# Graph network edge loops: streamed loads and stores for two chunks of edges at a time

## The chip, the cores and the metric

The kernel runs on one core of one Trainium2 chip. The metric is the device time of one execution in microseconds (us). Several executions are timed and the median is given. One further execution is recorded by the hardware profiler; its page and its trace are what is read here. A difference of about 0.2% (21 us) is what a measurement of this kernel can tell from no change.

## The reference

The reference computes two graph layers after one another on 10000 nodes with 64 features and 160000 edges that are sorted by their target node `dst`. The first is a GENConv stack of four layers with a softmax per target node and feature, the second is one attention layer. Cut to what matters:

```
h  = relu(layernorm(x));  x0 = h @ encW + encb;  ea = edge_attr @ eencW + eencb
genconv(x):                                   # four times, with layernorm and relu between
    m      = relu(x[src] + ea) + 1e-7
    logits = m * t
    e      = exp(logits - segment_max(logits, dst)[dst])
    agg    = segment_sum(m * e / segment_sum(e, dst)[dst], dst)
    return mlp(agg + x)
x = x + genconv stack(h)
attention:                                    # once
    score  = exp(clip(sum_per_head(K[src] * Q[dst] / sqrt(8) * E), -5, 5))
    x      = x + segment_sum(V[src] * score, dst)
```

The inputs are float32.

## The kernel before

**Tiling.** The sorted edge list is cut in the middle. The first half runs forwards on partitions 0 to 63 and the second half runs backwards on partitions 64 to 127, so one column of a tile holds one edge of each half, with 64 features each. A group is 128 columns and a chunk is four groups, 512 columns; 80000 columns make 158 chunks, of which the last three are shorter (`chunks`, `NC`). Sums and maxima per target node are scans along the columns; a row of marks in bfloat16 tells where a node's edges end or go on.

**Stages.** After a setup (encoder, marks, indices) come four softmax layers (`softmax_layer`, numbered 0 to 3), each followed by a node layer, then the attention layer and a last pass of gathers. Each softmax layer and the attention layer is one loop over the 158 chunks, in which most of the time lies. Between them the node layer gathers one row per node from the states (`n_g`) and builds the next table.

**One chunk of a softmax layer.** `front(k)` issues eight gathers on POOL (L650, 128 rows each, tile `xg` with seven buffers); multiplies the edge features on PE into the PSUM tile `z` (L734, three buffers) and adds the gathered rows in four further matmuls (L736); ACT turns `z` into logits (L739, L740); DVE scans them with the marks (L746) and subtracts (L748); ACT makes exponentials (L751 to L754, L761). `back(k)`, which is called one chunk later, makes two more scans on DVE (L774, L776, L779), transposes the results into the tile `so` (L805) and stores it in four transfers on SP's queue (L809).

**What is streamed on SP's queue.** `fetch(k + 2)` is called at the start of round `k`: the marks in two transfers (L709, five buffers) and the edge features `ea` in one (L660, three buffers). So one chunk of layers 1 to 3 issues seven transfers in this order: marks, marks, `ea` of chunk k+2, then four stores of chunk k-1. In layer 0 the edge features come as rows in two transfers (`er`, L667 and L669), are turned on PE (`turn_rows`, L678, L679), copied by ACT (L682) and written out as `eaT` (L683), which makes nine transfers.

**The attention layer** has the same form: `fetch_kv` issues eight gathers on POOL (`kv`, L650, in the same seven buffers as `xg`), `fetch(k + 2)` loads queries `q` (L1035), marks and `ea`; `ahead`, `scores`, `weights` and `back` compute, and `back` stores four transfers (L1110): eight transfers a chunk.

**What sets the order.** `InOrder` makes every engine run its instructions in the order in which the program issues them. Waits between engines are semaphores that the framework places. A transfer's completion counts on one of eight semaphores of its queue in turn, and each transfer waits until the transfer eight before it has landed.

Of the kernel before, what the change touches and what calls it, by code (L numbers as in the profile page):

```python
# [16 lines left out]
P = 128  # L17
# [4 lines left out]
CG = 4  # L22
# [4 lines left out]
def kernel(ctx: ExitStack, tc: tile.TileContext, a, out):  # L27
# [22 lines left out]

    chunks = [(g, CG) for g in range(0, NG - 5, CG)] + [(NG - 5, 2), (NG - 3, 2), (NG - 1, 1)]
    NC = len(chunks)
    W = 1280
    R = NE // W
    KT = W // P
# [617 lines left out]
    def turn_rows(k, er):  # L673

        g0, n, cols = span(k)
        pt = ps("ept", [P, CE])
        for g in range(n):
            nc.tensor.matmul(pt[:D, g * G:(g + 1) * G], er[:, 0, g, :], ident, start=True, stop=True)  # L678
            nc.tensor.matmul(pt[D:, g * G:(g + 1) * G], er[:, 1, n - 1 - g, :], anti,  # L679
                             start=True, stop=True)  # L680
        ea = edge.tile([P, CE], F32, name="ea", bufs=3)
        nc.scalar.activation(ea[:, :n * G], pt[:, :n * G], AF.Copy)  # L682
        nc.sync.dma_start(eaT[:, cols], ea[:, :n * G])  # L683
        return ea

    class InOrder:
# [14 lines left out]
                self.last[ins.engine] = ins  # L701
            self.seen = len(self.block.instructions)

    def load_marks(k, rows):

        g0, n, cols = span(k)
        t = edge.tile([P, CE], BF, name="marks", bufs=5)
        for s in range(2):
            nc.sync.dma_start(t[s * D:(s + 1) * D, :n * G], rows[s:s + 1, cols].to_broadcast([D, n * G]))  # L709
        return t  # L710
# [3 lines left out]
    def softmax_layer(l, ea_rows=None):  # L714
# [5 lines left out]
            numbers = ps("oe", [P, P])  # L720
            V.tensor_copy(numbers, iota_row)

        def fetch(k):
            return load_marks(k, ends_d), load_ea(k) if ea_rows is None else load_rows(k, ea_rows)

        def front(k, marks, ea):
            g0, n, cols = span(k)
            m = n * G
            xg = edge.tile([P, CG, 2, D], F32, name="xg", bufs=7)
            for g in range(n):  # L730
                for s in range(2):
                    gather(xg[:, g, s, :], tables[l], index(g0 + g, s))
            z = ps_a([P, CE])
            nc.tensor.matmul(z[:, :m], eencW, ea[:, :m], start=True, stop=False)  # L734
            for g in range(n):
                nc.tensor.matmul(z[:, g * G:(g + 1) * G], xg[:, g, :, :].rearrange("p s d -> p (s d)"),  # L736
                                 ident, start=False, stop=(g == n - 1))
            lg = ps("lg", [P, CE])
            S.activation(lg[:, :m], z[:, :m], AF.Relu)  # L739
# [30 lines left out]
        def back(k, z, u, dec, e):  # L770
# [35 lines left out]
            rows_out = st0[2 * g0 * G:2 * (g0 + n) * G, :].rearrange(  # L806
                "(b e s) (h x) -> s h e b x", e=32, s=2, h=2)
            for q in range(4):
                nc.sync.dma_start(rows_out[q // 2, q % 2],  # L809
                                  so[q * 32:(q + 1) * 32, :m // 32].rearrange("p b i c -> p b (i c)"))  # L810

        order = InOrder()
        got = [fetch(k) for k in range(2)]
        ea = got[0][1] if ea_rows is None else turn_rows(0, got[0][1])
        held, counts = None, []
        for k in range(NC):
            if k + 2 < NC:
                got.append(fetch(k + 2))
            z, u, up, e = front(k, got[k][0], ea)
            if k + 1 < NC:  # L820
                ea = got[k + 1][1] if ea_rows is None else turn_rows(k + 1, got[k + 1][1])
# [12 lines left out]
    def node_layer(l):  # L834
# [193 lines left out]
    def attention_layer():  # L1028

        prev = {}  # L1030

        def fetch(k):
            g0, n, cols = span(k)
# [3 lines left out]
            return load_marks(k, keeps_d), q, load_ea(k)  # L1037

        def ahead(k, keep, q, ea):

            g0, n, cols = span(k)
            m = n * G
            pq = ps("oe", [P, CE])
            for g in range(n):
                nc.tensor.matmul(pq[:, g * G:(g + 1) * G], q[:, g, :, :].rearrange("p s d -> p (s d)"),  # L1045
# [43 lines left out]
        def back(k, keep, pv, sc):  # L1089
            g0, n, cols = span(k)  # L1090
            m = n * G
            wv = ps("lg", [P, CE])
# [12 lines left out]
            so = edge.tile([P, CE // 32, 32], F32, name="so1", tag="so", bufs=3)  # L1105
            V.transpose(so[:, :m // 32, :], s[:, :m].rearrange("p (b e) -> p b e", e=32))
            rows_out = st1[2 * g0 * G:2 * (g0 + n) * G, :].rearrange(
                "(b e s) (h c) -> s h e b c", e=32, s=2, h=2)
            for q in range(4):
                nc.sync.dma_start(rows_out[q // 2, q % 2], so[q * 32:(q + 1) * 32, :m // 32])  # L1110

        order = InOrder()
        got = [fetch(k) for k in range(2)]
        made = ahead(0, *got[0])
        held = None
        for k in range(NC):
            kvs = fetch_kv(k)
            if k + 2 < NC:
                got.append(fetch(k + 2))
# [3 lines left out]
            held = got[k][0], pv, weights(k, psc)  # L1123
            if k + 1 < NC:
                made = ahead(k + 1, *got[k + 1])
            order()
        back(NC - 1, *held)
        order()
# [72 lines left out]
```

## Time and profile before

| | us |
|---|---|
| median of 3 runs | 10540.5 (10537.92 to 10543.13) |
| profiled execution, its own time | 10552.99 |
| its span on the core | 10551.1 |

The span by stage, from the first gather of each loop to its last, in windows of the trace (us):

| stage | window | length | POOL busy | DVE busy | PE busy | ACT busy |
|---|---|---|---|---|---|---|
| layer 0 | 160.6 to 2263.0 | 2102.4 | 1182.5 | 1241.8 | 832.2 | 622.4 |
| layer 1 | 2501.5 to 4270.7 | 1769.2 | 1182.2 | 921.4 | 565.3 | 540.6 |
| layer 2 | 4492.8 to 6262.7 | 1769.9 | 1182.2 | 922.1 | 565.5 | 540.9 |
| layer 3 | 6485.7 to 8258.9 | 1773.2 | 1182.3 | 921.1 | 563.6 | 540.1 |
| attention | 8616.6 to 10406.5 | 1789.9 | 1183.4 | 901.6 | 871.2 | 96.3 |

How to read it: the profiled execution took 12.5 us more than the median, so a sum that is made in the trace is taken to the median by leaving out 12.5 us. PE is TensorE, PEld its weight loads, DVE VectorE, ACT ScalarE, POOL GpSimd, SP SyncE; "SPq" marks a transfer that SP issues. An engine that is busy for half of a stage can still be the one that sets its length, when it also needs time between its instructions. "Remote" as the releaser of a wait means that the profile found no instruction or transfer that ended just then.

### The profile page before, as it was taken

How to read it: one execution, taken by the hardware profiler on the slowest of the kernel's cores; microseconds unless marked ns; L12 is line 12 of the kernel's file. 1: busy time of each engine (PE TensorE's matmuls, PEld its weight loads, DVE VectorE, ACT ScalarE, POOL GpSimd, SP SyncE). 2: the span in 40 equal slices, each digit the busy share in tenths (PEclk: the TensorE clock that was granted, in tenths of full speed). 3: DMA queues.
4: the chain of work that ended last, by engine and by line, in shares of the span. 5: the costliest groups of instructions: out<-in, count | busy, mean ns of one | idle time of the engine just before them, and what ended most of it. 6: DMA issues, size and time to landing. Idle time of an engine off the chain costs nothing. (4 is left out here: it accounts for less than half of the span.)

```text
span 10551.1 us, 67713 instructions
## 1 busy us (share of the span) xinstructions
PE 3999.8 (38%) x15722; PEld 2664.3 (25%) x15722; DVE 5487.0 (52%) x7537; ACT 2806.8 (27%) x4787; POOL 6367.8 (60%) x6736
## 2 busy tenths in 40 slices
PE   2433444344333333423333334233333355454452
PEld 1322322222222222212222222122222233333332
DVE  3666666642555555435555552555555445555553
ACT  1323333333333333423333333233333320000000
POOL 2555555545666666466666655666666456666665
PEclk8666666666555555655655556555555667777776
DMA  3545555454444444334444442444444325555553
GB/s 104 109 105 109 109 108 107 107 145 119 99 104 106 104 103 105 78 76 104 104 104 103 107 108 53 94 106 104 102 104 106 78 69 130 123 130 126 123 127 83
DMA packets 2467719, 1103.64 MB, mean 105 GB/s; under 512 B 2047265, under 2 KB 2239911, under 8 KB 2467088
## 3 DMA queue, kind: packets, MB, share of 16 engines
q1 hardware_dynamic: 2252120, 827.12, 33.5%
q0 software_dynamic: 215200, 272.11, 12.0%
q8 instruction: 140, 2.29, 0.1%
q14 instruction: 259, 2.12, 0.1%
HBM read 626.48 MB, written 471.91 MB: 104 GB/s over the span
## 5 line engine op out<-in xcount | busy, mean ns | idle before, releaser
L650 POOL DMA_INDIRECT xg<-table,idxA x2500 | 2364.8, 946 | 2198.2 <-issue 706.1
L734 PE MATMUL z<-ea,eencW 128*128 128x512 f32 (+1 forms) x1264 | 1271.0, 1108 | 4869.2 <-ACT ea L682 988.9
L650 POOL DMA_INDIRECT xg<-table,idxB x2500 | 2364.5, 946 | 763.6 <-issue 760.2
L746 DVE TENSOR_TENSOR_SCAN u<-lg,u,marks 128x512 f32<-128x512 f32 (+1 forms) x628 | 798.8, 1272 | 2962.3 <-ACT lg L740 2185.9
L734 PEld LDWEIGHTS z<-ea,eencW 128*128 128x128 f32 x1264 | 311.9, 306 | 5012.4 <-issue 2087.2
L736 PEld LDWEIGHTS z<-ident,xg 128*128 128x128 f32 x5000 | 1204.3, 329 | 747.6 <-issue 725.1
L736 PE MATMUL z<-ident,xg 128*128 128x128 f32 x5000 | 1186.1, 415 | 94.3 <-DMA xg<-table,idxB 77.5
L739 ACT ACTIVATE lg<-z 128x512 f32<-128x512 f32 (+1 forms) x632 | 356.8, 565 | 2689.1 <-remote 2112.7
L650 POOL DMA_INDIRECT kv<-kv_table,idxA x625 | 591.2, 946 | 414.9 <-remote 212.6
L776 DVE TENSOR_TENSOR_SCAN se<-dec,se,e 128x512 f32<-128x512 f32 (+1 forms) x628 | 791.9, 1261 | 0.0
L779 DVE TENSOR_TENSOR_SCAN sm<-dec,sm,me 128x512 f32<-128x512 f32 (+1 forms) x628 | 781.9, 1245 | 0.0
L751 ACT ACTIVATE up<-lg 128x512 f32<-128x512 f32 (+1 forms) x632 | 374.4, 592 | 1306.3 <-DVE lg L748 701.7
L650 POOL DMA_INDIRECT kv<-kv_table,idxB x625 | 591.2, 946 | 191.1 <-issue 189.3
L1079 PE MATMUL dec<-eq,head_sum 128*128 128x512 f32 (+2 forms) x316 | 238.0, 844 | 919.2 <-DVE eq L1077 879.9
L650 POOL DMA_INDIRECT n_g<-st,ends x316 | 301.9, 955 | 430.2 <-DMA marks<-ends_d 107.8
L1086 ACT ACTIVATE sc<-sc 128x512 f32<-128x512 f32 (+1 forms) x158 | 98.7, 625 | 1724.9 <-DVE sc L1085 660.4
L761 ACT ACTIVATE dec<-up 128x512 f32<-128x512 f32 (+1 forms) x632 | 376.8, 596 | 644.3 <-issue 540.0
L740 ACT ACTIVATE lg<-lg,teps,tcol 128x512 f32<-128x512 f32 (+1 forms) x632 | 471.8, 747 | 21.0
L1050 DVE TENSOR_TENSOR_SCAN qh<-marks,qh,oe 128x512 f32<-128x512 bf16 (+1 forms) x157 | 198.4, 1264 | 519.9 <-remote 429.2
L748 DVE TENSOR_TENSOR lg<-lg,u 128x512 f32<-128x512 f32 (+1 forms) x632 | 438.1, 693 | 22.0
L805 DVE STREAM_TRANSPOSE so<-se 128x512 f32<-128x512 f32 (+1 forms) x632 | 429.3, 679 | 0.0
L774 DVE SCALAR_TENSOR_TENSOR me<-z,e 128x512 f32<-128x512 f32 (+1 forms) x632 | 426.0, 674 | 0.0
(270 smaller groups left out, 6592.0 us busy)
## 6 DMA issues: line engine op xcount, KB each, us to landing
st<-so SPq DMA_DIRECT2D x2480, 128.0 KB
ea<-eaT SPq DMA_DIRECT2D x620, 256.0 KB
marks<-ends_d SPq DMA_DIRECT2D x1240, 64.0 KB
st<-so SPq DMA_DIRECT2D x652, 64.0 KB
xg<-table,idxA POOLq DMA_INDIRECT x2500
xg<-table,idxB POOLq DMA_INDIRECT x2500
qs<-zeros SPq DMA_DIRECT2D x156, 256.0 KB
er<-in_edge_attr_dram SPq DMA_DIRECT2D x310, 128.0 KB
```

The lines of the kernel that those rows point to most:

```text
L650: nc.gpsimd.indirect_dma_start(out=t, out_offset=None, in_=table, in_offset=bass.IndirectOffsetOnAxis(ap=idx, axis=0))
L734: nc.tensor.matmul(z[:, :m], eencW, ea[:, :m], start=True, stop=False)
L736: nc.tensor.matmul(z[:, g * G:(g + 1) * G], xg[:, g, :, :].rearrange("p s d -> p (s d)"), ident, start=False, stop=(g == n - 1))
L740: S.activation(lg[:, :m], lg[:, :m], AF.Identity, bias=teps[:, l:l + 1], scale=tcol[:, l:l + 1])
L746: V.tensor_tensor_scan(u[:, 1:m + 1], lg[:, :m], marks[:, :m], last, op0=OP.max, op1=OP.add)
L748: V.tensor_sub(lg[:, :m], lg[:, :m], u[:, 0:m])
L751: S.activation(up[:, :m], lg[:, :m], AF.Relu)
L761: S.activation(dec[:, :m], up[:, :m], AF.Exp, scale=-1.0)
L774: V.scalar_tensor_tensor(me[:, :m], z[:, :m], 0.0, e[:, :m], op0=OP.max, op1=OP.mult)
L776: V.tensor_tensor_scan(se[:, :m], dec[:, :m], e[:, :m], prev.get("e", zero1), op0=OP.mult, op1=OP.add)
L779: V.tensor_tensor_scan(sm[:, :m], dec[:, :m], me[:, :m], prev.get("m", zero1), op0=OP.mult, op1=OP.add)
L805: V.transpose(so[:, :m // 32, i, :], t[:, :m].rearrange("p (b e) -> p b e", e=32))
```

## The change

Chunks are joined to units of two (`units`, `unit_of`); the last two chunks are units of their own, so there are 80 units. The tiles of marks, edge features, rows, queries and stored states become twice as wide. `fetch` is called once for a unit, at the first chunk of the unit before it. `back` transposes each chunk into its half of `so` and issues the four stores at the last chunk of a unit; `turn_rows` does the same with the `eaT` store. Buffers, in units: marks three (from five chunks), `ea` three (from three chunks), `er` and `q` two (from three chunks), `so` two (from three chunks). The node layer's tile `n_g` takes the place of `ea` instead of that of `so`. The arithmetic and the gathers are as before, and the bytes of the transfers too.

For two chunks the transfers are: softmax layers 1 to 3 seven instead of fourteen, layer 0 nine instead of eighteen, attention eight instead of sixteen, each of twice the size.

```diff
+    units = [[k, k + 1] for k in range(0, NC - 2, 2)] + [[NC - 2], [NC - 1]]
+    unit_of = {k: u for u, ks in enumerate(units) for k in ks}
...
+    def reach(u):
+        g0 = chunks[units[u][0]][0]
+        n = sum(chunks[k][1] for k in units[u])
+        return g0, n, slice(g0 * G, (g0 + n) * G)
+    def within(k):
+        c = (chunks[k][0] - chunks[units[unit_of[k]][0]][0]) * G
+        return slice(c, c + chunks[k][1] * G)
...
-    def load_ea(k):
-        g0, n, cols = span(k)
-        ea = edge.tile([P, CE], F32, name="ea", bufs=3)
+    def load_ea(u):
+        g0, n, cols = reach(u)
+        ea = edge.tile([P, 2 * CE], F32, name="ea", bufs=3)
         nc.sync.dma_start(ea[:, :n * G], eaT[:, cols])
         return ea
-    def load_rows(k, ea_rows):
-        g0, n, cols = span(k)
-        er = edge.tile([P, 2, CG, D], F32, name="er", bufs=3)
+    def load_rows(u, ea_rows):
+        g0, n, cols = reach(u)
+        er = edge.tile([P, 2, 2 * CG, D], F32, name="er", bufs=2)
...
-        nc.scalar.activation(ea[:, :n * G], pt[:, :n * G], AF.Copy)
-        nc.sync.dma_start(eaT[:, cols], ea[:, :n * G])
+        nc.scalar.activation(ea[:, in_unit], pt[:, :n * G], AF.Copy)
+        if is_last(k):
+            nc.sync.dma_start(eaT[:, unit_cols], ea[:, :total * G])
...
-        t = edge.tile([P, CE], BF, name="marks", bufs=5)
+        t = edge.tile([P, 2 * CE], BF, name="marks", bufs=3)
...
-            so = edge.tile([P, CE // 32, 2, 32], F32, name="so", bufs=3)
+            if is_first(k):
+                prev["so"] = edge.tile([P, 2 * CE // 32, 2, 32], F32, name="so", bufs=2)
+            so, to = prev["so"], within(k)
             for i, t in ((0, se), (1, sm)):
-                V.transpose(so[:, :m // 32, i, :], t[:, :m].rearrange("p (b e) -> p b e", e=32))
+                V.transpose(so[:, to.start // 32:to.stop // 32, i, :],
+                            t[:, :m].rearrange("p (b e) -> p b e", e=32))
+            if not is_last(k):
+                return
...
-        got = [fetch(k) for k in range(2)]
+        got = [fetch(0)]
         for k in range(NC):
-            if k + 2 < NC:
-                got.append(fetch(k + 2))
-            z, u, up, e = front(k, got[k][0], ea)
+            if is_first(k) and unit_of[k] + 1 < len(units):
+                got.append(fetch(unit_of[k] + 1))
+            z, u, up, e = front(k, got[unit_of[k]][0], ea)
...
-            my["g"] = t = edge.tile([P, GRP, D2], F32, name="n_g", tag="so", bufs=3)
+            my["g"] = t = edge.tile([P, GRP, D2], F32, name="n_g", tag="ea", bufs=3)
...
-            q = edge.tile([P, CG, 2, D], F32, name="q", tag="er", bufs=3)
+            q = edge.tile([P, 2 * CG, 2, D], F32, name="q", tag="er", bufs=2)
```

The attention layer's `fetch`, `ahead` and `back` are changed in the same way.

More of the change, by code (lines that the diff above doesn't have):

```diff
@@ L655, in span, with is_first, is_last @@
         return g0, n, slice(g0 * G, (g0 + n) * G)
-    def load_ea(k):
-        g0, n, cols = span(k)
-        ea = edge.tile([P, CE], F32, name="ea", bufs=3)
+    def reach(u):
[5 more added lines that the diff above has]
+        return slice(c, c + chunks[k][1] * G)
+    def is_first(k):
+        return units[unit_of[k]][0] == k
+    def is_last(k):
+        return units[unit_of[k]][-1] == k
+    def load_ea(u):
+        g0, n, cols = reach(u)
+        ea = edge.tile([P, 2 * CE], F32, name="ea", bufs=3)
         nc.sync.dma_start(ea[:, :n * G], eaT[:, cols])
         return ea
-    def load_rows(k, ea_rows):
-        g0, n, cols = span(k)
-        er = edge.tile([P, 2, CG, D], F32, name="er", bufs=3)
+    def load_rows(u, ea_rows):
+        g0, n, cols = reach(u)
+        er = edge.tile([P, 2, 2 * CG, D], F32, name="er", bufs=2)
         e1 = NE - g0 * G
@@ L671, in load_rows, with turn_rows @@
         return er
-    def turn_rows(k, er):
+    def turn_rows(k, er, ea):
         g0, n, cols = span(k)
+        in_unit = within(k)
+        first, total, unit_cols = reach(unit_of[k])
+        at = g0 - first
         pt = ps("ept", [P, CE])
         for g in range(n):
-            nc.tensor.matmul(pt[:D, g * G:(g + 1) * G], er[:, 0, g, :], ident, start=True, stop=True)
-            nc.tensor.matmul(pt[D:, g * G:(g + 1) * G], er[:, 1, n - 1 - g, :], anti,
+            nc.tensor.matmul(pt[:D, g * G:(g + 1) * G], er[:, 0, at + g, :], ident, start=True, stop=True)
+            nc.tensor.matmul(pt[D:, g * G:(g + 1) * G], er[:, 1, total - 1 - at - g, :], anti,
                              start=True, stop=True)
-        ea = edge.tile([P, CE], F32, name="ea", bufs=3)
-        nc.scalar.activation(ea[:, :n * G], pt[:, :n * G], AF.Copy)
-        nc.sync.dma_start(eaT[:, cols], ea[:, :n * G])
+        if ea is None:
+            ea = edge.tile([P, 2 * CE], F32, name="ea", bufs=3)
+        nc.scalar.activation(ea[:, in_unit], pt[:, :n * G], AF.Copy)
+        if is_last(k):
+            nc.sync.dma_start(eaT[:, unit_cols], ea[:, :total * G])
         return ea
@@ L702, in __call__, with load_marks @@
             self.seen = len(self.block.instructions)
-    def load_marks(k, rows):
-        g0, n, cols = span(k)
-        t = edge.tile([P, CE], BF, name="marks", bufs=5)
+    def load_marks(u, rows):
+        g0, n, cols = reach(u)
+        t = edge.tile([P, 2 * CE], BF, name="marks", bufs=3)
         for s in range(2):
@@ L721, in softmax_layer, with fetch @@
             V.tensor_copy(numbers, iota_row)
-        def fetch(k):
-            return load_marks(k, ends_d), load_ea(k) if ea_rows is None else load_rows(k, ea_rows)
+        def fetch(u):
+            return load_marks(u, ends_d), load_ea(u) if ea_rows is None else load_rows(u, ea_rows)
         def front(k, marks, ea):
@@ L728, in front @@
             m = n * G
+            ea, marks = ea[:, within(k)], marks[:, within(k)]
             xg = edge.tile([P, CG, 2, D], F32, name="xg", bufs=7)
@@ L801, in back, with turn @@
                                            far[:, i:i + 1], op0=OP.mult, op1=OP.add)
-            so = edge.tile([P, CE // 32, 2, 32], F32, name="so", bufs=3)
+            if is_first(k):
+                prev["so"] = edge.tile([P, 2 * CE // 32, 2, 32], F32, name="so", bufs=2)
+            so, to = prev["so"], within(k)
             for i, t in ((0, se), (1, sm)):
-                V.transpose(so[:, :m // 32, i, :], t[:, :m].rearrange("p (b e) -> p b e", e=32))
-            rows_out = st0[2 * g0 * G:2 * (g0 + n) * G, :].rearrange(
+                V.transpose(so[:, to.start // 32:to.stop // 32, i, :],
+                            t[:, :m].rearrange("p (b e) -> p b e", e=32))
+            if not is_last(k):
+                return
+            first, total, _ = reach(unit_of[k])
+            rows_out = st0[2 * first * G:2 * (first + total) * G, :].rearrange(
                 "(b e s) (h x) -> s h e b x", e=32, s=2, h=2)
             for q in range(4):
-                nc.sync.dma_start(rows_out[q // 2, q % 2],
-                                  so[q * 32:(q + 1) * 32, :m // 32].rearrange("p b i c -> p b (i c)"))
+                nc.sync.dma_start(
+                    rows_out[q // 2, q % 2],
+                    so[q * 32:(q + 1) * 32, :total * G // 32].rearrange("p b i c -> p b (i c)"))
+        def turn(k, ea):
+            if ea_rows is None:
+                return got[unit_of[k]][1]
+            return turn_rows(k, got[unit_of[k]][1], None if is_first(k) else ea)
         order = InOrder()
-        got = [fetch(k) for k in range(2)]
-        ea = got[0][1] if ea_rows is None else turn_rows(0, got[0][1])
+        got = [fetch(0)]
+        ea = turn(0, None)
         held, counts = None, []
         for k in range(NC):
-            if k + 2 < NC:
-                got.append(fetch(k + 2))
-            z, u, up, e = front(k, got[k][0], ea)
+            if is_first(k) and unit_of[k] + 1 < len(units):
+                got.append(fetch(unit_of[k] + 1))
+            z, u, up, e = front(k, got[unit_of[k]][0], ea)
             if k + 1 < NC:
-                ea = got[k + 1][1] if ea_rows is None else turn_rows(k + 1, got[k + 1][1])
+                ea = turn(k + 1, ea)
             for c in counts:
@@ L1030, in attention_layer, with fetch @@
         prev = {}
-        def fetch(k):
-            g0, n, cols = span(k)
-            q = edge.tile([P, CG, 2, D], F32, name="q", tag="er", bufs=3)
+        def fetch(u):
+            g0, n, cols = reach(u)
+            q = edge.tile([P, 2 * CG, 2, D], F32, name="q", tag="er", bufs=2)
             nc.sync.dma_start(
                 q[:, :n], qs[2 * g0 * G:2 * (g0 + n) * G, :].rearrange("(g p s) d -> p g s d", p=G, s=2))
-            return load_marks(k, keeps_d), q, load_ea(k)
+            return load_marks(u, keeps_d), q, load_ea(u)
         def ahead(k, keep, q, ea):
@@ L1042, in ahead @@
             m = n * G
+            keep, ea = keep[:, within(k)], ea[:, within(k)]
+            q = q[:, within(k).start // G:within(k).stop // G]
             pq = ps("oe", [P, CE])
@@ L1091, in back @@
             m = n * G
+            keep = keep[:, within(k)]
             wv = ps("lg", [P, CE])
@@ L1104, in back @@
                                        op0=OP.mult, op1=OP.add)
-            so = edge.tile([P, CE // 32, 32], F32, name="so1", tag="so", bufs=3)
-            V.transpose(so[:, :m // 32, :], s[:, :m].rearrange("p (b e) -> p b e", e=32))
-            rows_out = st1[2 * g0 * G:2 * (g0 + n) * G, :].rearrange(
+            if is_first(k):
+                prev["so"] = edge.tile([P, 2 * CE // 32, 32], F32, name="so1", tag="so", bufs=2)
+            so, to = prev["so"], within(k)
+            V.transpose(so[:, to.start // 32:to.stop // 32, :], s[:, :m].rearrange("p (b e) -> p b e", e=32))
+            if not is_last(k):
+                return
+            first, total, _ = reach(unit_of[k])
+            rows_out = st1[2 * first * G:2 * (first + total) * G, :].rearrange(
                 "(b e s) (h c) -> s h e b c", e=32, s=2, h=2)
             for q in range(4):
-                nc.sync.dma_start(rows_out[q // 2, q % 2], so[q * 32:(q + 1) * 32, :m // 32])
+                nc.sync.dma_start(rows_out[q // 2, q % 2], so[q * 32:(q + 1) * 32, :total * G // 32])
         order = InOrder()
-        got = [fetch(k) for k in range(2)]
+        got = [fetch(0)]
         made = ahead(0, *got[0])
@@ L1117, in attention_layer @@
             kvs = fetch_kv(k)
-            if k + 2 < NC:
-                got.append(fetch(k + 2))
+            if is_first(k) and unit_of[k] + 1 < len(units):
+                got.append(fetch(unit_of[k] + 1))
             pv, psc = scores(k, kvs, made)
@@ L1122, in attention_layer @@
                 back(k - 1, *held)
-            held = got[k][0], pv, weights(k, psc)
+            held = got[unit_of[k]][0], pv, weights(k, psc)
             if k + 1 < NC:
-                made = ahead(k + 1, *got[k + 1])
+                made = ahead(k + 1, *got[unit_of[k + 1]])
             order()
```

## The prediction

> **What bounds the kernel now.** The page comes first: its engine shares and its costliest groups.
>
> ```profile
> span 10551.1 us, 67713 instructions
> PE 3999.8 (38%) x15722; PEld 2664.3 (25%) x15722; DVE 5487.0 (52%) x7537; ACT 2806.8 (27%) x4787; POOL 6367.8 (60%) x6736
> L650 POOL DMA_INDIRECT xg<-table,idxA x2500 | 2364.8, 946 | 2198.2 <-issue 706.1
> L739 ACT ACTIVATE lg<-z 128x512 f32<-128x512 f32 (+1 forms) x632 | 356.8, 565 | 2689.1 <-remote 2112.7
> ```
>
> The busiest engine, POOL, has 60%, but its gathers need more than their 946 ns: in the timeline below one starts 1.25 us after the other (0.95 and 0.30 of "issue"). Eight a chunk make 10.0 us. The loops take 1769.2/158 = 11.2 us a chunk in layer 1, 11.3 in attention and 13.3 in layer 0; the other engines stay below (DVE 921.4/158 = 5.8). So POOL sets the length of each loop, and beyond its 1.25 us a gather only its pauses can be gained.
>
> The second view is the list of waits, cut to the stretch of layers 1 to 3:
>
> ```profile
> ACT lg L739 <- remote: 2080.1, 171, 21.0
> POOL xg L650 <- remote: 657.4, 160, 12.5
> ```
>
> and the same list for POOL in attention and in layer 0:
>
> ```profile
> POOL kv L650 <- remote: 212.6, 68, 5.9
> POOL xg L650 <- PE z L736: 528.1, 74, 8.9
> ```
>
> The third is the timeline, for what "remote" hides. One pause, near the end of layer 1:
>
> ```profile
> 4014.28 4.23 SPq L809 DMA_DIRECT2D st<-so  x4
> 4014.28 1.92 PE L736 MATMUL z<-ident,xg 128*128 128x128 f32 x8
> 4016.86 0.94 POOL L650 DMA_INDIRECT xg<-table,idxB  x1 [0.30 <-issue]
> 4019.23 1.40 SPq L709 DMA_DIRECT2D marks<-ends_d  x2
> 4020.70 0.58 ACT L739 ACTIVATE lg<-z 128x512 f32<-128x512 f32 x1 [8.91 <-remote]
> 4020.93 0.94 POOL L650 DMA_INDIRECT xg<-table,idxA  x1 [3.12 <-remote]
> ```
>
> PE has finished `z` at 4016.2. ACT, which waits for it, starts at 4020.70, 4.5 us later, and POOL 0.2 us after ACT: a gather waits until PE has used the buffer seven chunks back. In all 158 pauses over 0.8 us of layers 1 to 3, PE's record of the `z` that POOL waits for ends at least 12 us before the pause. So PE isn't late; the word of it is. It arrives after POOL has stood still for some 3 us and SP has got rid of its transfers, which meanwhile leave every 1.40 us (marks: two issues in 2.8 us at 4061.53) where they take 0.55 otherwise (stores, four in 2.19 at 4058.77). I read this as a stretch of gathers that holds back signals, and a pause that lets them through. What holds them, no view shows.
>
> The trace's instructions, counted pause by pause, give the price. Layers 1 to 3: 158 pauses, 670.2 us, mean 4.24. By the number of SP issues inside: two, 3.30 us (36 pauses); three, 3.79 (63); four, 5.21 (46); five, 5.56 (5). From two to five that is (5.56 - 3.30)/3 = 0.75 us an issue, and the mean pause meets 3.0 issues. Attention has 93 pauses, 253.8 us, mean 2.74; 92 of them meet no issue. Layer 0 has 84, 563.2 us, mostly 7.65.
>
> **Part by part.**
>
> *Fewer issues in the pauses of layers 1 to 3.* Seven transfers for two chunks take the place of fourteen. If a pause then meets half as many, 1.5 instead of 3.0, it is 1.5 x 0.75 = 1.1 us shorter: 1.1 x 158 = 178 us less. One bound is zero (issues only fall into pauses, they don't make them). The other is attention's pause without issues: (4.24 - 2.74) x 158 = 237, and 265 if pauses also get rarer by a tenth. Nearest is the slope, from pauses of these very loops: -178.
>
> *Does an issue of twice the bytes cost twice?* The nearest rows say no: at 9015.24 attention issues four stores of 64 KB in 1.97 us (0.49 each), layer 1 four of 128 KB in 2.19 (0.55); a 256 KB load of `ea` takes 0.53 at 4055.70, two marks of 64 KB at least 1.17. Taken: the price of one. The upper bound, twice, is the first rival.
>
> Here the Trainium skill weighs in ("DMA: Bandwidth & Descriptors", Specifications): below 512 bytes a piece a transfer doesn't reach full rate. The page counts 2047265 of 2467719 packets under 512 B, and stores stay in 256-byte pieces at either size. If piece count were what stores cost, only the three loads of a unit's seven transfers would gain: 178 x 3/7 = 76 us instead of 178. No trace row shows the rate of one piece.
>
> *Layer 0.* A pause here is a chain: PE's `ept` comes through 2.9 us into the pause, then ACT copies (L682), PE makes `z` and POOL goes on, 7.65 in all. SP's issues follow the release, so I take 0. Bounds: 1.1 x 84 = 95 us either way. The `eaT` store leaves once for two chunks; it is read a layer later.
>
> *Attention.* 92 of 93 pauses meet no issue: 0; bound 1 x 0.75 x 93 = 70 us either way.
>
> *Moved transfers.* SP's queue becomes: marks, marks, `ea` of unit u+1, four stores of unit u-1. The fetch stands behind the stores of unit u-2, whose transposes end in the first round of unit u-1, and its data is wanted by PE's `z` of the next unit's first chunk, at the earliest a round later: 10 us of lead. Before, `ea` already came late for PE at times, the list of waits has 75 such ("PE z L734 <- DMA ea<-eaT: 448.7, 75, 8.2"), and these lie under the 12 us by which `z` is early. Cost 0; without that cover a late load costs its lateness, 6 us (448.7/75) for each of 80 units at most of a layer. The stores wait for the second `so` transpose; behind them on SP stands only the next fetch. In attention `q` moves likewise.
>
> *Buffers.* Two units of `so`, `er`, `q` are four chunks for three, three of `ea` six for three, three of marks six for five. A unit's `so` is written again two units later: 20 us after its store was issued. Cost 0.
>
> *Loop starts.* The first `ea` is 512 KB for 256; the first eight gathers (10 us) cover it. `n_g` in the buffers of `ea`: each stage has left these tiles before the node layer begins. Cost 0; bound, four node layers by one 256 KB landing of some 5 us = 20 us.
>
> *Arithmetic.* PE, ACT, DVE and POOL run the same instructions in the same order: 0.
>
> Sum: 10552.99 - 178 = 10375 for the profiled execution, and less its 12.5 us over the median **10362 us**.
>
> The clock of TensorE doesn't enter: the windows give a granted clock of 0.56 in layer 1 and PE is 12 us early. On increments the skill has a figure ("TensorE: Matmul & The Clock Gate", The cost: per-tile semaphore tail): they follow one another at 26.3 ns. By it, five of a chunk would be late by 0.13 us, and the change could gain nothing in pauses; the row at 4020.70 shows 4.5 us, and the measurement decides.
>
> **The rivals.**
>
> *Slower: the doubled transfers cost by their bytes.* Then an issue inside a pause takes 1.5 us, and the join brings all seven together: a release that comes after SP has got rid of its group waits for a longer group. At 1.5 issues met this is no change; at 2.0, (2.0 x 1.5 - 3.0 x 0.75) x 158 = +118, 10,659; at 2.25, +178, 10,718; at 3.0, +355, 10,896. It decides from more than 1.5 met on. For it: pauses with four issues last 5.21, and groups of up to seven now stand in a row. Against it: the sizes of 64, 128 and 256 KB at one price above.
>
> *No change: POOL and PE alone set the pause.* Attention pauses 2.74 us with SP silent, and three issues (3.79) cost little more than two (3.30); the issues may merely fill a pause that would be there. 10,540, within 20.
>
> *Much faster: SP's traffic causes the hold-back.* With half of it, pauses vanish to the 0.30 of an issue: 670 - 158 x 0.30 = 623 less, 9,917. Against it: attention's pauses with SP silent, and layer 3's start, where with SP nearly idle one `z` reached ACT 20.99 us after the last (at 6575.23).
>
> **How the numbers follow.** Forecast 0.56; bytes 0.24; no change 0.12; vanishing pauses 0.08. A measurement of this kernel can tell some 0.2%, 21 us, from nothing. Faster by more: 0.56 + 0.08 = 0.64; same: 0.12; slower: 0.24. The forecast's own range runs from -265 and layer 0's -95 (10,180) to near no change. The range goes from there up to 10,660, the bytes rival at 2.0 issues met: left out are the vanishing pauses (0.08) and half of the bytes rival (0.12), 0.20 in all.
>
> **What would show it.** Right: POOL's gathers still 1.25 us apart; layers 1 to 3 at about 1769 - 59 = 1710 each; some 158 pauses of 3.1 us mean with 1.5 issues; layer 0 and attention within 1% of 2102 and 1790; SP's issues 0.5 to 1.4 us each, as before. Wrong: stores of 256 KB that take 1 us or more each outside pauses (bytes); pauses as long as before with fewer issues in them (no change); the same pauses but many more of them; or a new wait of PE's `z` for `ea` in the pauses' place, with `z` no longer 12 us early, which would mean that the joined fetch is late.

## The result, and the profile after

The changed kernel took 10580.8 us (median of 7 runs, 10563.8 to 10599.4) where the kernel before took 10543.1 in the same comparison: a ratio of 1.0032, with a 95% interval of 1.0022 to 1.0043. A second comparison (`after_again`) gave 1.0036 (1.0022 to 1.0050). So the change makes the kernel about 0.35% slower, some 38 us, where 178 us less had been forecast.

The page of the changed kernel, which took 10599.4 us in its profiled execution:

```profile
span 10597.6 us, 62122 instructions
PE 3983.5 (38%) x15722; PEld 2655.1 (25%) x15722; DVE 5491.1 (52%) x7537; ACT 2809.3 (27%) x4787; POOL 6352.8 (60%) x6736
L653 POOL DMA_INDIRECT xg<-table,idxA x2500 | 2359.0, 944 | 2231.9 <-remote 703.8
L765 ACT ACTIVATE lg<-z 128x512 f32<-128x512 f32 (+1 forms) x632 | 358.0, 566 | 2695.6 <-remote 2072.3
st<-so SPq DMA_DIRECT2D x1232, 256.0 KB
ea<-eaT SPq DMA_DIRECT2D x308, 512.0 KB
marks<-ends_d SPq DMA_DIRECT2D x616, 128.0 KB
```

The change did what it says: half as many transfers of twice the size, the same compute instructions. But the idle time of the gathers (L653) and of ACT's first step (L765) is what it was. The waits in layers 1 to 3, in the form waiting engine, tile, line, releaser: total, times, longest:

```profile
ACT lg L765 <- remote: 2042.2, 197, 21.0
POOL xg L653 <- remote: 702.3, 169, 13.1
PE z L760 <- DMA ea<-eaT: 137.0, 23, 11.1
```

POOL waits 702 us where it had waited 657. The last line is a gain that brought nothing: PE's waits for `ea` in these layers fell to 137.0 us from the 425.2 of before:

```profile
PE z L734 <- DMA ea<-eaT: 425.2, 69, 8.2
```

The timeline of one pause of the changed kernel:

```profile
3926.61 4.13 SPq L841 DMA_DIRECT2D st<-so  x4
...
3930.79 3.53 SPq L734 DMA_DIRECT2D marks<-ends_d  x2
3931.86 1.91 PE L762 MATMUL z<-ident,xg 128*128 128x128 f32 x8
...
3934.41 0.53 SPq L680 DMA_DIRECT2D ea<-eaT  x1
...
3944.11 0.94 POOL L653 DMA_INDIRECT xg<-table,idxB  x1 [0.30 <-issue]
3948.68 0.58 ACT L765 ACTIVATE lg<-z 128x512 f32<-128x512 f32 x1 [15.74 <-remote]
3948.92 0.94 POOL L653 DMA_INDIRECT xg<-table,idxA  x1 [3.86 <-remote]
```

SP has issued its last transfer at 3934.41, ten microseconds before POOL stops, and is silent in the whole pause. PE's last `z` ended at 3933.8. Yet ACT, which waits for a `z`, starts at 3948.68, and the pause is 3.86 us. Counted over layers 1 to 3: 170 pauses, 704.7 us, mean 4.15; 116 of them meet no issue at all, and their mean is 4.12. The mean number of issues met fell from 3.0 to 0.66, and the pauses stayed.

The same timeline shows that an issue became dearer. The four stores of 256 KB took 4.13 us and the two marks 3.53. Counted over layers 1 to 3, the mean issue of a store rose from 0.59 us to 1.00 and that of a marks transfer from 0.63 to 1.64; within a group of four stores it was the third and the fourth that rose, from 0.60 and 0.72 to 1.36 and 1.73. In all, SP issued for 1732 us where it had issued for 1829. So half the number of issues saved 5% of their time.

### The profile page after: what moved, and what is told of

It is laid out like the page before. It is cut to its first block, busy times and chain, and to the rows that moved or that the text cites. A ratio compares the mean times of both kernels' runs of the same rounds, so it can differ in the third digit from the quotient of the medians.

```text
span 10597.6 us, 62122 instructions
## 1 busy us (share of the span) xinstructions
PE 3983.5 (38%) x15722; PEld 2655.1 (25%) x15722; DVE 5491.1 (52%) x7537; ACT 2809.3 (27%) x4787; POOL 6352.8 (60%) x6736
## 4 chain that ended last, share of the span: by engine, by line
another core or an unknown queue 30%; DVE 19%; issue 15%; ACT 14%; PE 11%; POOL 8%; DMA 2%; SPq 1%; DVEq 0%; ACTq 0%; POOLq 0%
POOL xg L653 7%; DVE u L772 5%; ACT lg L766 3%; PE z L760 3%; DVE lg L774 2%; ACT lg L765 2%; PE z L762 2%; ACT up L777 2%; DVE sm L805 2%; ACT dec L787 2%; DVE se L802 2%; ACT e L780 2%; ACT e L779 1%; PE z L1114 1%
## 5 line engine op out<-in xcount | busy, mean ns | idle before, releaser
L653 POOL DMA_INDIRECT xg<-table,idxA x2500 | 2359.0, 944 | 2231.9 <-remote 703.8
L760 PE MATMUL z<-ea,eencW 128*128 128x512 f32 (+1 forms) x1264 | 1247.1, 1088 | 4926.0 <-DVE me L800 1257.0
L653 POOL DMA_INDIRECT xg<-table,idxB x2500 | 2359.2, 944 | 766.7 <-issue 756.7
L762 PEld LDWEIGHTS z<-ident,xg 128*128 128x128 f32 x5000 | 1181.3, 323 | 736.2 <-issue 716.4
L762 PE MATMUL z<-ident,xg 128*128 128x128 f32 x5000 | 1164.6, 409 | 98.8 <-DMA xg<-table,idxB 78.7
L765 ACT ACTIVATE lg<-z 128x512 f32<-128x512 f32 (+1 forms) x632 | 358.0, 566 | 2695.6 <-remote 2072.3
L653 POOL DMA_INDIRECT kv<-kv_table,idxA x625 | 589.6, 943 | 431.6 <-remote 246.0
L653 POOL DMA_INDIRECT kv<-kv_table,idxB x625 | 589.8, 944 | 191.3 <-issue 191.3
L653 POOL DMA_INDIRECT n_g<-st,ends x316 | 301.2, 953 | 436.3 <-issue 208.5
```

The costliest lines, as they stand in the source:

```text
L653: nc.gpsimd.indirect_dma_start(out=t, out_offset=None, in_=table, in_offset=bass.IndirectOffsetOnAxis(ap=idx, axis=0))
```

## The experiments

The chips differ, and the numbers can't be read without that: in three of the five comparisons the kernel before took 10,533 to 10,554 us (medians), as in the first times; in the other two, on other chips, 8,850. The ratios are each against the kernel before on the same chip. Each chip served in one comparison only, so that what is called a kind of chip below could also be something that was set up for that comparison. The second kind is used as an experiment of its own below.

The stages, from the first gather of a loop to its last, from the traces (us); "rest" is the span less the five loops:

| kernel | layer 0 | layer 1 | layer 2 | layer 3 | attention | rest |
|---|---|---|---|---|---|---|
| before, first trace | 2102 | 1769 | 1770 | 1773 | 1790 | 1347 |
| changed, first trace | 2119 | 1778 | 1776 | 1779 | 1804 | 1342 |
| before_again | 2058 | 1778 | 1778 | 1779 | 1809 | 1344 |
| after_again (same chip) | 2118 | 1777 | 1774 | 1777 | 1802 | 1335 |
| loads_pair | 2127 | 1778 | 1775 | 1779 | 1798 | 1350 |
| stores_pair (same chip) | 2129 | 1785 | 1784 | 1786 | 1807 | 1354 |
| nostore_again | 2056 | 1773 | 1772 | 1773 | 1807 | 1314 |
| xg_10 | 2051 | 1780 | 1778 | 1779 | 1815 | 1442 |
| rest_512 | 2052 | 1783 | 1788 | 1784 | 1821 | 1349 |
| rest3_l0_again | 1848 | 1822 | 1819 | 1822 | 1840 | 1220 |
| pair_layer0 | 2122 | 1771 | 1772 | 1773 | 1791 | 1334 |
| pair_later (same chip) | 2103 | 1768 | 1768 | 1769 | 1789 | 1337 |
| paced_l0 (same chip) | 1837 | 1782 | 1782 | 1781 | 1802 | 1207 |
| split_st, other kind of chip | 1560 | 1560 | 1560 | 1560 | 1562 | 1058 |

### Are SP's transfers what makes a pause?

**Half of the change each.** The edit of `loads_pair` leaves the stores of each chunk alone; `stores_pair` joins those and leaves the loads:

```diff
 loads_pair, against the changed kernel
-            if not is_last(k):
-                return
-            first, total, _ = reach(unit_of[k])
+            so = edge.tile([P, CE // 32, 2, 32], F32, name="so", bufs=3)
 stores_pair, against the kernel before
+            if is_first(k):
+                prev["so"] = edge.tile([P, 2 * CE // 32, 2, 32], F32, name="so", bufs=2)
+            if not is_last(k):
+                return
```

> Only the loads (marks, edge features, rows, queries) come two chunks at a time; the stores stay as before. The changed kernel took 38 us more than before (10581 against 10543). Theory 1, long runs of stores keep the gathers' packets waiting (in the changed kernel's trace no gather packet moves for some 3 us while four 256 KB stores run): no loss here, 10,540 within 20. Theory 2, the cost comes with joined loads (512 KB of edge features at once): 10,570 to 10,590. If fewer issues in the pauses were worth anything after all, loads give 3/7 of 178: 10,465.

> Only the stores of the states are joined to two chunks; the loads stay as before. Theory 1, runs of four 256 KB stores hold up the gathers: the whole loss is here, 10,565 to 10,590. Theory 2, the loads: 10,540 within 20. By the price of an issue of the prediction: 4/7 of 178 less, 10,440.

Measured: loads alone 1.0051 (1.0038 to 1.0065), stores alone 1.0090 (1.0074 to 1.0105). Neither gains, so no price of an issue shows, for loads or for stores. Each half loses more than the whole did on other chips, which no theory had. The table shows layer 0 at 2127 and 2129 with either half; the further 10 us a layer of `stores_pair` are not explained.

**No stores in layers 1 to 3.**

```diff
+            if l > 0:
+                return
             rows_out = st0[2 * g0 * G:2 * (g0 + n) * G, :].rearrange(
```

> Layers 1 to 3 store no states (layer 0's stand in for them, so this part of the result is left out). On a chip with pauses: if stores' packets or issues make the pauses, the 222 us a layer fall by 80 or more; if POOL's gathers alone do, 1769 us a layer within 10. On a chip without pauses: 1560 us a loop, as before.

Measured: 0.9960 (0.9946 to 0.9975), 35 us less, for the most part not in the loops. Four of seven transfers and their 512 KB a chunk are gone, and layers 1 to 3 take 1772 to 1773 us for before_again's 1778, their pauses 226 to 229 us for 230. Most of the gain lies in the stretches between the loops (1314 for 1344). In the three layers SP issued for 633 us where before_again has 1781. So neither the number of issues nor their time nor the packets of the stores make the pauses.

### Do more buffers shorten the pauses?

```diff
-            xg = edge.tile([P, CG, 2, D], F32, name="xg", bufs=7)
+            xg = edge.tile([P, CG, 2, D], F32, name="xg", bufs=10)
```

> The kernel before with ten buffers for gathered rows instead of seven. Theory A (a fixed rate, 1.43 us a gather): runs get longer and pauses too, time the same, 10,540 within 40. Theory B (a pause is a fixed 3 to 5 us that ends a run): runs of seven chunks in place of four, pauses rarer by a third or more, 0.33 x 670 = 220 less in layers 1 to 3, about 10,320.

Measured: 1.0092 (1.0077 to 1.0107). The pauses of a layer sum to 228 to 230 us, as with seven buffers; a run of gathers is still mostly four chunks and then waits 5.7 us. What is lost lies between the loops (1442 for about 1345): more chunks are left over when the gathers of a loop end (in layer 1 the next gather follows after 78.0 us, in before_again after 57.2).

Nearly the same sum in every case (219 to 244 us for each of layers 1 to 3, in all traces without memsets on chips with pauses) points to a fixed share for each gather. The first trace of before has it too, if a pause is set against the run ahead of it: four chunks (32 gathers) and 5.6 us where such runs follow one another, 0.175 us a gather; four chunks and 4.2, then one chunk and 3.0, again 7.2/40 = 0.18. The start of the loop doesn't fit: 104 gathers and only 12 us, 0.12 a gather. In all, 222 us for 1250 gathers, 0.18 on average. A share for each chunk of eight gathers would look the same; no run tells the two apart.

### Does it help to slow POOL down?

One memset after each chunk's gathers, and then three:

```diff
+            for _ in range(3):
+                nc.gpsimd.memset(rest, 0.0)
```

> The kernel before with one extra instruction on POOL after the eight gathers of each chunk, a memset of 128x512 that nothing reads (some 0.6 us and 0.3 between instructions, estimated). Theory A, a limit on the rate (gathers and their pauses together always come to 1.43 us a gather): pauses get shorter by what is inserted, 10,540 within 40. Theory B, a long unbroken run of gathers is what holds PE's signals back: short breaks let them through, pauses vanish and a chunk of layers 1 to 3 takes 10.0 + 0.9 instead of 11.4, 0.5 x 158 x 3 = 237 less, about 10,300. Theory C, pauses are set by something else and the insert is added to them: 0.9 x 790 = 710 more, 11,250.

Measured: 1.0025 (1.0015 to 1.0035). From the last gather of a chunk to the next lie 0.71 us with the memset and 0.30 without (medians where there is no pause), so layers 1 to 3 got 0.40 x 158 = 63 us of extra work each (the expectation of `rest3_all` counts 0.30 a chunk, which is too little). Their pauses, with the memsets that lie in them, fell from 230 us to between 188 and 194, and the loops are 5 to 10 us longer than before_again: most is absorbed.

> Three memsets of 128x512 on POOL after each chunk's gathers in all five loops. On a chip with pauses, theory A (a backlog of 0.178 us a gather, worked off while POOL issues no gather): layers 1 to 3 within 1% of 1770 us, their pauses gone (under 60 us beyond the memsets), layer 0 at 1820 to 1860 instead of 2102, about 10,300 in all. Theory C (pauses come whatever the breaks): each loop up to 240 us longer. On a chip without pauses: 1.6 x 158 = 253 a loop more, as before, 10,115.

(All five loops have the three memsets.) Measured: 0.9845 (0.9827 to 0.9863), 162 us less, with more work on the engine that bounds the kernel. The timeline of a chunk:

```profile
5013.10 0.96 POOL L652 DMA_INDIRECT xg<-table,idxB  x1 [0.30 <-issue]
5014.05 1.70 POOL L736 MEMSET rest<- 128x512 f32 x3
5015.93 0.95 POOL L652 DMA_INDIRECT xg<-table,idxA  x1 [0.17 <-issue]
```

and the largest waits in layers 1 to 3:

```profile
PE z L740 <- DMA xg<-table,idxB: 2658.5, 1554, 5.3
...
POOL xg L652 <- issue: 1095.3, 3575, 39.0
```

No "remote" wait of POOL or of ACT's L743 is left; 1554 times PE waits for a gather to land, as it should where POOL is the bound. ACT's first step in these layers starts 0.04 us (median) after the end of PE's `z`, where it was 12.0 in the kernel before. Between the last gather of a chunk and the next lie 1.88 us (median; 1.87 in the timeline), 1.58 more than the 0.30 of an issue; the old pauses came to 1.42 a chunk. That fits theory A, with layer 0 at 1848 (expected 1820 to 1860), where the pauses had been longer. Layers 1 to 3 missed it: at 1819 to 1822 they are 2.8 to 3.0% over the 1770 of the expectation, which had said 1%. The stretches between the loops are 124 us shorter, as less is held back when a loop ends: after layer 1 the next gather follows after 15.6 us instead of 57.2.

### Where are the 38 us of the change made?

The two traces on one chip, before_again and after_again, put it in layer 0: 59.6 us more there, 21.8 less in everything else.

> The changed kernel once more. On the chip of the experiments before these, the kernel before took 8850 us where it had taken 10,540 to 10,554, and its gathers ran 1.248 us apart without a pause in layers 1 to 3. Theory R (the loss is made in the pauses): on a chip with pauses again 0.2% to 0.5% slower; on a chip without them there is nothing to lengthen, and the times agree within 0.2%. Theory F (the loss comes from the fetches of double size, at loop starts and ends): 20 to 40 us more on either chip.

> The kernel before, unchanged, for a trace on the same chip as the changed one. If the chip is without pauses: gathers 1.25 us apart, 1560 us a loop, and PE's z signal reaches ACT within 0.3 us of the end of its matmuls. If it is one with pauses: 10,550 and 670 us of pauses in layers 1 to 3, as in the first trace.

That chip turned out to have the pauses; the other kind of chip is seen below. Then each part of the loops by itself:

```diff
 pair_layer0, against the kernel before
-            softmax_layer(0, ea_s)
+            softmax_layer_0(0, ea_s)      # layer 0's functions of the changed kernel
 pair_later, against the changed kernel
-            softmax_layer(0, ea_s)
+            softmax_layer_0(0, ea_s)      # layer 0's functions of the kernel before
```

> Layer 0 with its loads and stores two chunks at a time, all else as before. The changed kernel's two traces have layer 0 at 2119 and 2118 us, the kernel before 2102 and 2058; layers 1 to 3 differ by under 5 us each from the second trace of before. Theory L (the loss is made in layer 0, whose runs of gathers are locked to two chunks by the pairs): layer 0 at about 2120, the whole 20 to 50 us slower than before. Theory W (loss spread over all loops): about a third of it, 10 to 15 us.

> Layer 0 as before; loads and stores two chunks at a time in layers 1 to 3 and attention. Theory L: the same as before within 20 us. Theory W: 20 to 30 us slower. By the prediction's price of an issue: 178 us faster.

Measured: layer 0 alone 1.0024 (1.0014 to 1.0034), 27 us more; the later loops alone 0.9985 (0.9976 to 0.9994), 15 us less, which is under the 21 us that a measurement can tell from no change. So on this chip layer 0 loses and the later loops don't. That the whole 38 us come from layer 0 is not shown: the two parts add up to 0.1%, the whole change costs 0.32 to 0.36% on other chips, and in the first pair of traces 17 of 47 us lie in layer 0 and 35 in the later loops, with 5 less in the rest. The waits of POOL in layer 0, before_again and then after_again:

```profile
POOL xg L650 <- PE z L736: 433.8, 63, 8.7
```

```profile
POOL xg L653 <- PE z L762: 560.2, 74, 13.1
```

In layer 0 POOL runs for one chunk and then pauses some 2.6 us, or for two and pauses 7.6 to 7.8: 12.6 or 13.8 us a chunk. Before_again has 48 runs of one and 49 of two; after_again 6 and 70; `pair_layer0` none and 73. The layer 0 of before drifts between both kinds: its first trace has 16 and 65, and 2102 us, and `pair_later`, which has the same layer 0, 14 and 66, and 2103. In all five traces on these chips with pairs in layer 0, be it of loads, of stores or of both, 67 to 73 runs are of two chunks and the layer takes 2118 to 2129. What in the pairs holds it there is not shown. Some 9.5 us of the extra length lie at the start of the layer, which with joined loads begins 11 to 12 us earlier: in the first traces a pause of 3.9 us after the first gather and one of 13.0 after the 64th, where before has one of 7.4.

### A chip without the pauses

> The kernel before with each store of states cut in two along the blocks (64 KB in place of 128, eight stores a chunk in place of four, the same bytes and 256-byte pieces). If the number of SP's issues lengthened the pauses (0.75 us an issue): 4/7 of 3.0 more issues in each of 158 pauses, 1.7 x 0.75 x 158 = 200 more, 10,740. If long runs of store packets are what costs (stores joined: 93 more): the same or up to 40 less, 10,500 to 10,550. If neither counts: 10,545 within 20.

Measured: 1.0018 (1.0009 to 1.0027), on a chip on which the kernel before takes 8850 us. Every loop of this run takes 1560 to 1562: 1250 gathers, 1.248 us apart, and but for one of 2.1 us no pause. So this run couldn't test the pauses; four more issues a chunk cost 16 us, none of it in the loops (the unchanged loops of `rest3_l0` take 1560 to 1562 too). On such a chip also:

> Layers 1 to 3 store no states (the states of layer 0 stand in for them, so this part of the result is left out); loads as before, three issues a chunk in place of seven, 512 KB a chunk less to move. If SP's issues make the pauses: the mean pause falls from 4.24 to about 2.7, 80 us less a layer. If the stores' packets do, by holding up the gathers: pauses fall too, by up to as much. If a limit of POOL's gathers alone sets the rate: 1.41 to 1.42 us a gather, 1769 us a layer within 10.

0.9964 (0.9949 to 0.9978): the loops stay at 1560, the 32 us lie between them.

> The kernel before with three memsets of 128x512 on POOL after each chunk's gathers, in all five loops. One of them added 0.30 us a chunk in layers 1 to 3; three should add some 1.5 (0.30 and twice 0.6). Theory A (a backlog that grows with every gather and is worked off only while POOL issues none, 0.178 us a gather or 1.42 a chunk): layers 1 to 3 keep their 1770 us, their pauses fall from 222 us to under 60, and layer 0, whose pauses lie in a chain of ACT and PE, falls from 2102 to about 1850. Theory C (a pause costs its 4 us whenever POOL has run ahead of PE's signals, whatever the breaks): each loop gets 1.5 x 158 = 237 us longer.

> The same three memsets in layer 0 alone. Theory A: some 250 us less than before, about 10,300. Theory C: 237 more, 10,790. One memset everywhere had taken layer 0 from 2102 to 2052.

1.1431 (1.1413 to 1.1448) and 1.0282 (1.0267 to 1.0298): here the memsets only cost, 253 to 259 us a loop. The loops with them take 1815 to 1819 us, within 2% of the same kernel's on the chip with pauses (1819 to 1848). Slowed to this pace, the two kinds of chip nearly agree.

> Layer 0 alone with its loads and stores two chunks at a time, a second time, for the spread between chips: 10 to 60 us slower than before, layer 0 at 2115 to 2125 and in runs of two chunks, whatever layer 0 of before does (2058 or 2102).

0.9995 (0.9986 to 1.0004): where there are no pauses, the pairs in layer 0 lose nothing (1565 us for 1560, and an earlier start). So their loss shows only where there are pauses. On this chip the signal comes at once; its timeline:

```profile
2007.33 0.80 PE L738 MATMUL z<-ident,xg 128*128 128x128 f32 x2 [1.71 <-DMA xg<-table,idxB]
...
2008.16 0.58 ACT L741 ACTIVATE lg<-z 128x512 f32<-128x512 f32 x1 [3.03 <-PE z L738]
```

PE ends at 2008.13 and ACT starts 0.03 us later, where it was 4.5 us and more before.

### A version that beats both on a chip with pauses

POOL is paced only where its pauses cost more than the pacing: in layer 0, and at the end of the other loops.

```diff
+    def rest(k, paced):
+        sizes = [512] * 5 if k >= NC - 9 else [512, 512, 317] if paced else []
+        for w in sizes:
+            nc.gpsimd.memset(spare[:, :w], 0.0)
...
+            rest(k, l == 0)
```

> The kernel before with POOL slowed to about 11.45 us a chunk by memsets after the gathers of each chunk (two of 128x512, one of 128x317), and five of 128x512 in the last nine chunks of each loop, so that nothing is held back when the loop ends. Theory A (a backlog of some 1.42 us a chunk): no pauses are left to add, loops of about 1810, layer 0 too, node layers 40 us shorter as with three memsets, 10,220 to 10,300. If 11.45 is still too fast, pauses come back in part and layer 0 stays near 2050: 10,450.

> The kernel before with POOL paced in the same way in layer 0 only, and five memsets of 128x512 in the last nine chunks of the other loops. Theory A: layer 0 at about 1830 in place of 2060 to 2100, the node layers 40 us shorter, layers 1 to 3 as before plus a few us: 10,180 to 10,260.

Measured: paced everywhere 0.9801 (0.9787 to 0.9816), in layer 0 and at the ends 0.9682 (0.9668 to 0.9696), 10194 us. Between chunks lie 1.88 us as with three full memsets, so the narrower third one saves nothing. Layer 0 takes 1837 us; POOL is busier there than in before_again and the layer shorter, in the windows' columns length, PE, PEld, DVE, ACT and POOL busy, clock, DMA share and GB/s, before_again and then `paced_l0`:

```profile
161.30:2219.20 2057.90, 833.76 (x5196) 601.68 (x5196) 1240.87 (x1787) 622.42 (x1053) 1182.34 (x1250) 0.65 0.49 107
```

```profile
161.00:1997.90 1836.90, 856.96 (x5230) 613.09 (x5230) 1253.05 (x1802) 630.21 (x1065) 1414.33 (x1737) 0.67 0.56 121
```

> The changed kernel with POOL paced as in the run paced_l0: memsets after each chunk's gathers in layer 0 (two of 128x512, one of 128x317), five of 128x512 in the last nine chunks of the other loops. If the change loses its time through the pauses of layer 0, the loss is gone where they are gone, and what pair_later gained stays: layer 0 at about 1837 as in paced_l0, the whole 10,160 to 10,200. If it loses in another way (joined fetches that come late): layer 0 at 1857 or more, 10,215 to 10,240.

This ran on a chip without pauses and gave 1.0396 (1.0382 to 1.0410), 350 us more, so its question stays unanswered; and it shows that the pacing is worth its price only on a chip that pauses.

## Why the prediction was wrong, point by point

**What bounds the kernel: right, but not finished.** POOL sets each loop, PE is early and its signal is late: all of that held. The pauses were read for what lies inside them and not for what lies ahead of them.

**Fewer issues in the pauses: this is the step that failed.** The slope of 0.75 us an issue was taken for a price. It also left out eight pauses that met no issue or one, among them the three longest (9.5 to 12.5 us, at the starts of the loops); over all 158 the slope is 0.40. The likely reading is the reverse one, which no run tests by itself: SP goes on issuing while POOL waits, so a longer pause holds more issues. The issues met did fall, further than forecast (0.66 for 1.5), and the mean pause went from 4.24 to 4.15, its sum from 670 to 705. In place of the price the runs show pauses that come to 0.18 or 0.19 us a gather on average, with half the issues, without stores and with ten buffers alike. The rival "POOL and PE alone set the pause" came nearest, at 0.12. (The bound of 265 doesn't follow from its terms either: a tenth fewer pauses of 2.74 us each give 281.)

**Twice the bytes at the price of one: wrong too, though it did not decide.** An issue took 1.12 us on average in layers 1 to 3 where it had taken 0.59, so SP's time hardly fell. Outside the pauses a store of 256 KB took 0.95 us, next to the 1 us that was to speak for the rival by bytes. The row that seemed to settle it, 0.53 us for 256 KB, was a load of `ea`; its packets are of 2 KB and a store's of 256 bytes, and whether size, pieces or the place in a group set the price no run separates. The rival had this premise and the sign of the result, but not the cause: it needed more than 1.5 issues in a pause and there were 0.66, and with a third of the issuing time in `nostore_again` the pauses stayed. The Trainium skill advises joining many small transfers into one large one, and calls those under 64 KB mostly overhead ("DMA: Bandwidth & Descriptors", Rules for kernel authors). Nearly all transfers joined here were of 64 to 256 KB; joined, they lost 0.24% in layer 0 alone and made no difference above 0.2% in the later loops.

**Layer 0 at zero: mis-sized.** The bound was 95 us either way; measured are 17 us (first traces), 20 (the chip of `pair_layer0`) and 60 (the chip of after_again) more. The argument that SP's issues follow the release says nothing of how many chunks POOL runs between pauses, and on the last two of these chips that is what changed.

**Attention, moved transfers, buffers, loop starts: near zero, as said.** Attention lost 14 us in the first pair of traces and gained 8 in the second. PE's waits for `ea` shrank and brought nothing, as the prediction had them covered. The stretch between layer 3 and attention took 7 to 10 us more, the time up to the first gather 11 to 12 less. No row shows the 5 us of a 256 KB landing in the bound for the loop starts; in layers 1 to 3 of before the packets of an `ea` load ended at most 3.3 us after its issue.

## What to carry to other kernels

A count of what lies inside a stall is no price: what goes on beside a stall piles up in a long one. Set the stall against the work ahead of it first; if stall time per piece of work is the same in different patterns, look for a limit on the rate; here only an even pace helped. The price of a larger transfer is read where that transfer stands, behind others of its kind: a larger one of another shape says little. An engine that runs ahead in bursts can lose more in a dependent chain than it wins, as POOL did in layer 0, so pacing it is worth one experiment, and a second chip is worth one before it is kept.

## What the runs showed of the hardware that was not expected

The same program took 10,506 to 10,562 us on some chips and 8,850 on others. A single gather took the same on both (1.25 us from one to the next), and so, by the median, did the main instructions of PE, ACT and DVE. On the slower chips PE's finished `z` reaches ACT only many microseconds later after a run of gathers (at least 14.9 in the pause shown; 12.0 by the median of layers 1 to 3 of before, 0.04 in `split_st`), and each of layers 1 to 3 takes some 1.42 us a gather, be it with pauses alone or with one memset a chunk (1.43). With three memsets a chunk it takes 1.46, and the signal is no longer late. The gathers' data are not what is behind: in layer 1 of before the last packet of a gather ends 2.2 us after the gather starts (median; 3.6 at most), and in `split_st`, without pauses, it is 2.2 and 3.4. On SP an issue of a store of 256 KB took 1.01 us and one of 128 KB 0.53, in layer 0 and layers 1 to 3 of `pair_layer0_again`. Which part of the chip is behind the limit, and why chips differ in it, no run here shows.
